# Gated scan and top-2 mixture of experts in fp32: the output products of an expert as seven block products, and one accumulator bank for z

## The chip, the core and the metric

The kernel runs on one core of one Trainium2 chip. The metric is the device time in microseconds (us) of one execution, lower is better; the time of a version is the median of its runs. A profile is one further execution, recorded instruction by instruction.

## The reference, cut to what matters

Two layers, each with a residual, on x of shape (8, 1024, 256), all in fp32. The first is a normalised gated linear scan. The second is a mixture of experts: 8 groups of 1024 tokens, 8 experts, each token goes to its two best experts, and each expert takes C = 256 places per group.

```
x = x + attn(layernorm(x))                 # projections, scan along the tokens
xn = layernorm(x)
expert_inputs  = einsum('GSEC,GSM->EGCM', dispatch, xn)         # M = 256
hidden         = gelu(einsum('EGCM,EMH->EGCH', expert_inputs, w0)) * einsum('EGCM,EMH->EGCH', expert_inputs, w1)
expert_outputs = einsum('EGCH,EHM->EGCM', hidden, wo)           # H = 1368
x = x + einsum('EGCM,GSEC->GSM', expert_outputs, combine)
```

The change is in the line of expert_outputs.

## The kernel before, in words

**Blocks, units, sets.** The 8 groups are worked in 4 blocks (n = 0 to 3) of 2 groups. A unit is one expert on one block, 32 units in all. H = 1368 is 11 chunks of 128 channels (the last has 88), and a set is two chunks of a unit: 6 sets per unit, s = 0 to 5, where s = 5 has the one chunk of 88. That makes 192 sets, worked in order by `run_set`. A *product* below is one `nc.tensor.matmul`; in fp32 it is two TensorE instructions in the trace.

**The w0 and w1 products.** For the two weights and the two groups, `run_set` forms four results with seven block products instead of eight (a Strassen-like scheme in Winograd's form). The sums of weights come from GpSimd (`row_sums`), the sums of inputs from VectorE (`column_sums`). Three of the partial results share one accumulating bank, z: TensorE writes `z a11`, ScalarE copies the bank to SBUF (snap0), TensorE adds `z s2`, ScalarE copies (snap1), TensorE adds `z s3`, ScalarE copies (snap2), TensorE adds `z a22`, and VectorE reads the bank a last time. Each step must wait until the copy before it is done. Other products stand between the steps: `p_a`, `p_b`, and the output products of the set before.

**The output products.** `outputs(st, part)` is called four times per set (group 0 or 1, first or second 128 places), each time with one product per chunk, so eight products in a full set and four in s = 5. It uses hid with places on the output partitions, so that the result in bank py is already stored as rows. The products of one set are issued in the next one: part 0 ahead of `z s2`, part 1 ahead of `z s3`, parts 2 and 3 ahead of `z a22`.

**VectorE in a set,** in the order written: c11 = snap0 + p_a (L750), the second gate of the set before (L729, completes group 1 of hid), snap2 + p_b (L766), the last read of z (L772, completes group 0 of hid), snap1 + p_b (L722).

**Everything else is fed in by `pump`,** twice per set: ahead of parts 2 and 3, and at the end. The list `plan` gives steps of the next block's attention, routing and gating (blocks 0 to 2), of the combination of the block before (blocks 1 to 3), and at fixed sets `gather_unit`, `input_channels` (transposes of the next unit's inputs, s = 3 and 4) and `column_sums` (at the end of s = 4 and in the middle of s = 5). One step can put up to 8 one-hot comparisons (L452) on VectorE. From the first set on the order on every engine is the written one (`manual_schedule`), and each engine works its own queue in that order.

**PSUM** has eight banks: z 2, pa 1, pb 1, py 2, aside 2 (transposes and everything from `pump`).

Of the kernel before, what the change touches and what calls it, by code (L numbers as in the profile page):

```python
# [8 lines left out]
FP = mybir.dt.float32  # L9
# [8 lines left out]
def kernel(  # L18
# [11 lines left out]
    nc = tc.nc  # L30
# [30 lines left out]

    BANKS = {"z": 2, "pa": 1, "pb": 1, "py": 2, "aside": 2}

    def bank(tag, name):
        return psum.tile([P, 512], FP, tag=tag, name=name, bufs=BANKS[tag])

# [5 lines left out]
    def ps_first(name):  # L72
        turn[0] += 1
        return bank(("z", "py", "pa", "z", "py", "pb")[turn[0] % 6], name)

# [4 lines left out]
    nc.scalar.dma_start(wr, router_w.rearrange("(c p) e -> p c e", p=P))  # L80
    wq_sb = pa.tile([P, 3 * KC, D], FP, tag="wq_sb", name="wq_sb")

# [6 lines left out]
    def load_w(b, e, s):  # L89
        lo, w = s * 2 * P, SW[s]  # L90
        a = wpool.tile([P, 2, KC, 2 * P], FP, tag="w01", name=f"w01_{b}_{e}_{s}")
        nc.sync.dma_start(a[:, 0, :, :w], w0[e, :, lo : lo + w].rearrange("(k p) h -> p k h", p=P))
        nc.sync.dma_start(a[:, 1, :, :w], w1[e, :, lo : lo + w].rearrange("(k p) h -> p k h", p=P))
        return a
# [10 lines left out]
    with tc.manual_schedule(engines={mybir.EngineType.SP}):  # L105
        xts = {0: load_x(0)}
        nc.sync.dma_start(wq_sb, w_qkva.rearrange("(c p) d -> p c d", p=P))
        for u in range(1, 3):
            xts[u] = load_x(u)
# [27 lines left out]
    for k in range(KC):  # L137
        for half in range(2):
            pw = ps_first(f"pw_{k}_{half}")
            for c in range(3):  # L140
                nc.tensor.transpose(
                    pw[:, c * P : (c + 1) * P],
                    wq_sb[:, half * 3 + c, k * P : (k + 1) * P],
                    ident,
                )
            nc.scalar.activation(
                wT[:, k, half * 3 * P : (half + 1) * 3 * P], pw[:, : 3 * P],
                AF.Copy, scale=gam[:, k : k + 1],
            )
# [44 lines left out]
    def unit_steps(u, ps):  # L194
# [86 lines left out]
        def second_norm():  # L281
            xn = pa.tile([P, UT, D], FP, tag="xn", name=f"xn_{u}", bufs=2)
            scale_rows(xn, xts.pop(u), t["mv"], t["r"][:, 0, :])
            nc.sync.dma_start(
                xn_d[b][hf * U : (hf + 1) * U, :].rearrange("(i p) d -> p i d", p=P), xn
            )
            t["xn"] = xn
# [32 lines left out]
    def gate_steps(n):  # L320
# [57 lines left out]
        def positions():  # L378
            m, mc = v["m"], v["mc"]
            pos_ps = ps_a(f"pos_{n}")[:, : 2 * T * NE]  # L380
            v["pos_ps"] = pos_ps
            nc.tensor.matmul(pos_ps, lhsT=before, rhs=m.rearrange("p r t e -> p (r t e)"),
                             start=True, stop=False)
            nc.tensor.matmul(pos_ps, lhsT=ones, rhs=mc[:, :, :, :TPG, :], start=False, stop=True)
            cnt_ps = ps_a(f"cnt_{n}")
            nc.tensor.matmul(cnt_ps[:, : GB * NE], lhsT=ones, rhs=mc[:, 0, :, TPG, :],
                             start=True, stop=True)
            cnt = ten("cnt", [P, GB, NE])
            V.tensor_scalar(cnt.rearrange("p g e -> p (g e)"), cnt_ps[:, : GB * NE],
                            float(CAP), None, ALU.min)  # L390

# [62 lines left out]

        def tokens(gl, part):
            tn = v["tn"]
            if part == 0:
                v["ptok"] = ps_a(f"ptok_{n}_{gl}")
            ptok = v["ptok"]
            for q in range(part * 8, part * 8 + 8):  # L460
                r, j = divmod(q, TPG)
                at = hot.pop((gl, q))
                for hh in range(NH):
# [5 lines left out]
                    )  # L469
            if part == 1:  # L470
                pk = ptok[:, : NH * 2 * NE].rearrange("p (h k e) -> p h k e", h=NH, k=2)
                td = pg.tile([P, NH, NE], FP, tag="td", name=f"td_{n}_{gl}")
                V.tensor_scalar(td, pk[:, :, 0, :], float(P), None, ALU.mult)
                V.tensor_tensor(tok[n][:, gl], td, pk[:, :, 1, :], ALU.add)

        steps = [softmax, softmax_sum, lambda: top(0), lambda: top(1), counts, positions, places]
        parts = [(gl, q) for gl in range(GB) for q in range(2)]
        ahead = [lambda gl=gl, q=q: one_hot(gl, q) for gl, q in parts]
        prods = [lambda gl=gl, q=q: tokens(gl, q) for gl, q in parts]
        steps.append(ahead[0])  # L480
        for i in range(len(parts)):
            if i + 1 < len(parts):
                steps.append(ahead[i + 1])
            steps.append(prods[i])
        return steps

    def combine_steps(n):
# [4 lines left out]
        def spare_rows():  # L492

            r = []
            for pool, tag, k in ((pb, "xc", 2), (pa, "h", 1), (pa, "oT", 1), (pa, "xnT", 1)):
                for i in range(k):
                    t = pool.tile([P, UT, D], FP, tag=tag, name=f"far_{tag}_{i}", bufs=k)
                    r += [t[:, q, :] for q in range(UT)]
# [54 lines left out]
    def last_expert_steps():  # L553
# [14 lines left out]
        def by_slot(u, j):  # L568
            if j == 0:
                places_of[u] = pa.tile(  # L570
                    [P, NH, U], FP, tag=("hT", "xn")[(u - lo) // 2], name=f"places_{u}", bufs=2
                )
# [15 lines left out]
    def add_last_expert(u, ot):  # L588
        b, hf = divmod(u, UPG)
        for j in range(2):  # L590
            pc = bank(("z", "aside")[j], f"pc_{u}_{j}")
            for i in range(2):
# [60 lines left out]
    def row_sums(j):  # L653
# [11 lines left out]
        sums[j] = a11, a12, a22, s1, s2, s3, s4  # L665

    class Set:

# [25 lines left out]
    ys = {}  # L694

    def outputs(st, part):

        gl, hh = divmod(part, 2)
        n, e, s, hs = st.n, st.e, st.s, st.hs
        if part % 2 == 0 and s == 0:  # L700
            ys[n, e, gl] = bank("py", f"py_{n}_{e}_{gl}")
        po = ys[n, e, gl]
# [6 lines left out]
        if part % 2 == 1 and s == NS - 1:  # L709
            g = n * GB + gl  # L710
            ot = pb.tile([P, NH, D], FP, tag="ot", name=f"ot_{n}_{e}_{gl}")
            nc.scalar.copy(ot.rearrange("p h d -> p (h d)"), ys.pop((n, e, gl)))
            if (n, e) == units[-1]:
                ys[gl] = ot
                return
            nc.sync.dma_start(
                y_d[g][e * CAP : (e + 1) * CAP, :].rearrange("(h p) d -> p h d", p=P), ot
            )

    def first_sum(st):  # L720
# [9 lines left out]

    def run_set(j, last, pump):

# [4 lines left out]
        nm = f"{st.n}_{st.e}_{st.s}"  # L737
        z, p_a = bank("z", f"z_{nm}"), bank("pa", f"pa_{nm}")
        st.hid = pb.tile([P, GB, 2, CAP], FP, tag="hid", name=f"hid_{nm}", bufs=3)
        st.h2 = st.hid.rearrange("p g c s -> p g (c s)")  # L740
        zz = st.cut(z)

        st.mm(z, a11, b11, True)
# [7 lines left out]
        if last:  # L751
            second_gate(last)
        if last:
            outputs(last, 0)
        st.mm(z, s2, t2, False)
        st.snap1 = st.ten("snap", "sn1", 4)
        A.copy(st.snap1, zz)  # L757
        A.activation(c11, c11, AF.Gelu_apprx_tanh)
        p_b = st.pb = bank("pb", f"pb_{nm}")
        st.mm(p_b, s1, t1, True)  # L760
        if last:
            outputs(last, 1)
        st.mm(z, s3, t3, False)
        snap2 = st.ten("snap", "sn2", 4)
        A.copy(snap2, zz)  # L765
        V.tensor_tensor(st.h2[: st.hs, 1, st.wide], snap2, st.cut(p_b), ALU.add)  # L766
        pump()
        if last:
            outputs(last, 2)
            outputs(last, 3)  # L770
        st.mm(z, a22, t4, False)
        V.tensor_tensor(st.h2[: st.hs, 0, st.wide], zz, c11, ALU.mult)  # L772
        st.mm(p_b, s4, b22, False)
        first_sum(st)
        pump()
        return st

# [65 lines left out]
    with tc.manual_schedule():  # L843
        last, late = None, [[] for _ in range(UB)]
        for n in range(NB):
# [6 lines left out]
            if n > 0:  # L852
                for i, (fetch, add) in enumerate(combine_steps(n - 1)):
                    plan.setdefault(6 + 5 * i, []).append(fetch)
                    plan.setdefault(8 + 5 * i, []).append(add)
            if n == NB - 1:
                for i, f in enumerate(last_expert_steps()):
                    plan.setdefault(8 + 2 * i, []).append(f)
                for i, (fetch, add) in enumerate(combine_steps(n)):
                    k = PUMPS - 2 * NS + 2 + i * 10 // 16  # L860
                    plan.setdefault(k, []).append(fetch)
                    if k + 5 < PUMPS - 1:
                        plan.setdefault(k + 5, []).append(add)
# [4 lines left out]
            def pump():  # L868
# [5 lines left out]
                if nxt in units:  # L874
                    if half == 0 and s == 0 and e + 1 < NE:
                        gather_unit(*nxt)
                    if half == 1 and s == 3:
                        input_channels(*nxt, 0)
                    if half == 0 and s == 4:
                        input_channels(*nxt, 1)  # L880
                    if s == (4, 5)[1 - half]:
                        column_sums(*nxt, 1 - half)
                at[0] += 1

            for j in range(n * NE * NS, (n + 1) * NE * NS):
                if j + 1 < len(sets):
                    row_sums(j + 1)
                st = run_set(j, last, pump)
                load_set(j + AHEAD)
# [39 lines left out]
```

## Time and profile before

| what | value |
|---|---|
| median of 3 runs | 2067.75 us (2064.25 to 2068.35) |
| the profiled execution | 2035.41 us, span 2033.6 us |
| mean granted TensorE clock in it | 0.99 |
| TensorE matmuls busy | 1994.8 us (98%), 9412 instructions |
| VectorE, ScalarE, GpSimd busy | 1056.7, 632.6 and 866.3 us |
| output products (L704) | 2816 instructions, 706.0 us |
| w0/w1 products into z, pa and pb (L682) | 4928 instructions |

How to read it: engines are named PE (TensorE matmul), PEld (TensorE weight load), DVE (VectorE), ACT (ScalarE), POOL (GpSimd) and SP. Matmuls overlap, so the duration of one (381 ns for 256 columns) is longer than the distance from one to the next. Row "idle before" of a group of instructions is the time in which the engine stood still just before them.

### The profile page before, as it was taken

What the parts mean: (1) busy time and instruction counts of PE and PEld (TensorE: products, weight loads), DVE (VectorE), ACT (ScalarE), POOL (GpSimd) and SP (SyncE); (2) the same over time, 40 slices, a digit from 0 to 9 for tenths busy, and PEclk for the clock granted to TensorE, in tenths of its full rate; (3) what the DMA queues carried; (4) which work ended last, traced back from release to release, by engine and by line L of the source; (5) the groups of instructions that cost most, each with busy time, mean ns of one, the idle gap of its engine ahead of it and who ended that gap; (6) DMA issues with size and microseconds to landing.
All of it is one profiled execution on the core that took longest, in us unless ns stands there. A gap on an engine that the chain in (4) does not pass through costs nothing.

```text
span 2033.6 us, 26826 instructions
## 1 busy us (share of the span) xinstructions
PE 1994.8 (98%) x9412; PEld 1658.4 (82%) x9412; DVE 1056.7 (52%) x2114; ACT 632.6 (31%) x1188; POOL 866.3 (43%) x1150
## 2 busy tenths in 40 slices
PE   8889999999999999999999999999999999999998
PEld 4568888888888888888788888888888888888887
DVE  4565354456545454546644554545564454554455
ACT  3222333332333322333332333333322333333331
POOL 2333243333334443545433454444433454444546
PEclk9889999999999999999999999999999999999999
DMA  5231433323332433443423344243334334253433
GB/s 181 73 114 54 123 109 94 111 76 99 103 103 91 135 98 115 134 126 112 148 68 99 124 130 135 80 144 105 116 107 119 119 112 136 86 161 100 139 119 99
DMA packets 224052, 228.80 MB, mean 113 GB/s; under 512 B 32432, under 2 KB 215728, under 8 KB 223920
## 3 DMA queue, kind: packets, MB, share of 16 engines
q1 hardware_dynamic: 211088, 193.51, 31.1%
q0 software_dynamic: 12288, 33.57, 5.7%
q8 instruction: 77, 1.26, 0.3%
q14 instruction: 55, 0.45, 0.1%
q10 hardware_dynamic: 544, 0.01, 0.0%
HBM read 185.61 MB, written 41.42 MB: 112 GB/s over the span
## 4 chain that ended last, share of the span: by engine, by line
PE 93%; DVE 4%; issue 1%; POOL 1%; ACT 1%; DMA 0%; ACTq 0%; DVEq 0%
PE z L682 29%; PE py L704 29%; PE pb L682 15%; PE pa L682 7%; PE pa L235 2%; PE pkv L235 2%; PE pq L235 2%; PE pl L301 1%; PE px L630 1%; PE po L268 1%; PE pc L594 1%; PE pt_h L185 1%; PE pt_x L185 1%; DVE oneh L452 0%; DVE y L255 0%
## 5 line engine op out<-in xcount | busy, mean ns | idle before, releaser
L704 PE MATMUL py<-wo,hid 128*128 128x256 f32 (+1 forms) x2816 | 706.0, 381 | 8.3 <-DVE hid L729 4.8
L704 PEld LDWEIGHTS py<-wo,hid 128*128 128x128 f32 (+1 forms) x2816 | 529.1, 190 | 99.0 <-issue 14.3
L661 POOL TENSOR_TENSOR sb<-w 128x256 f32<-128x256 f32 x188 | 129.5, 689 | 764.6 <-PE pb L682 758.7
L766 DVE TENSOR_TENSOR hid<-sn,pb 128x512 f32<-128x512 f32 x192 | 123.3, 642 | 535.4 <-ACT sn L765 534.4
L682 PE MATMUL z<-tb,sb 128*128 128x256 f32 (+1 forms) x1408 | 366.8, 379 | 0.1
L682 PEld LDWEIGHTS z<-tb,sb 128*128 128x128 f32 (+1 forms) x1408 | 262.7, 187 | 39.8 <-POOL sb L663 0.5
L745 ACT COPY sn<-z 128x512 f32<-128x512 f32 x192 | 105.4, 549 | 598.3 <-PE z L682 598.3
L772 DVE TENSOR_TENSOR hid<-z,c 128x512 f32<-128x512 f32 x192 | 123.7, 644 | 176.7 <-PE z L682 175.9
L750 DVE TENSOR_TENSOR c<-sn,pa 128x512 f32<-128x512 f32 x192 | 122.5, 638 | 128.4 <-PE pa L682 91.3
L757 ACT COPY sn<-z 128x512 f32<-128x512 f32 x192 | 105.3, 549 | 257.7 <-PE z L682 257.7
L682 PE MATMUL z<-xT,w 128*128 128x256 f32 (+1 forms) x704 | 184.9, 381 | 0.0
L682 PE MATMUL z<-tb,w 128*128 128x256 f32 (+1 forms) x704 | 184.6, 381 | 0.2 <-ACT sn L765 0.2
L682 PE MATMUL pb<-tb,sb 128*128 128x256 f32 (+1 forms) x704 | 183.3, 379 | 0.0
L682 PE MATMUL pa<-xT,w 128*128 128x256 f32 (+1 forms) x704 | 183.3, 379 | 0.0
L682 PE MATMUL pb<-xT,sb 128*128 128x256 f32 (+1 forms) x704 | 183.3, 379 | 0.0
L765 ACT COPY sn<-z 128x512 f32<-128x512 f32 x192 | 105.2, 548 | 215.1 <-PE z L682 215.1
L682 PEld LDWEIGHTS z<-tb,w 128*128 128x128 f32 (+1 forms) x704 | 130.6, 187 | 22.7 <-ACT sn L765 3.9
L682 PEld LDWEIGHTS pb<-tb,sb 128*128 128x128 f32 (+1 forms) x704 | 131.6, 187 | 20.3
L682 PEld LDWEIGHTS pa<-xT,w 128*128 128x128 f32 (+1 forms) x704 | 131.7, 187 | 20.3
L682 PEld LDWEIGHTS pb<-xT,sb 128*128 128x128 f32 (+1 forms) x704 | 131.6, 187 | 20.4
L682 PEld LDWEIGHTS z<-xT,w 128*128 128x128 f32 (+1 forms) x704 | 126.8, 188 | 24.8 <-issue 9.1
L729 DVE TENSOR_TENSOR hid<-hid,c 128x512 f32<-128x512 f32 x192 | 143.4, 747 | 3.3 <-ACT c L725 3.3
(150 smaller groups left out, 2312.4 us busy)
## 6 DMA issues: line engine op xcount, KB each, us to landing
w<-in_L_ffn_w_kernel_dram SPq DMA_DIRECT2D x320, 256.0 KB
wo<-in_L_ffn_wo_kernel_dram SPq DMA_DIRECT2D x160, 256.0 KB
y<-ot SPq DMA_DIRECT2D x62, 256.0 KB
xt<-in_L_attn_x_dram SPq DMA_DIRECT2D x16, 512.0 KB
x<-xt SPq DMA_DIRECT2D x16, 512.0 KB
xn<-xn SPq DMA_DIRECT2D x16, 512.0 KB
xc<-x SPq DMA_DIRECT2D x16, 512.0 KB
out_dram<-xc SPq DMA_DIRECT2D x12, 512.0 KB
```

The costliest lines, as they stand in the source:

```text
L185: nc.tensor.transpose(pt[:, i * P : (i + 1) * P], src[:, i, k * P : (k + 1) * P], ident)
L235: nc.tensor.matmul(pp, lhsT=wT[:, k, c * P : (c + 1) * P], rhs=t["hT"][:, k, :], start=(k == 0), stop=(k == KC - 1),)
L661: eng.tensor_tensor(s1, a21, a22, ALU.add)
L682: nc.tensor.matmul(ps[:hs, i * CAP : (i + 1) * CAP], lhsT=a[:, i * hs : (i + 1) * hs], rhs=b, start=first and i == 0, stop=True, skip_grou ...
L704: nc.tensor.matmul(po[:, hh * D : (hh + 1) * D], lhsT=st.hid[:hs, gl, i, hh * P : (hh + 1) * P], rhs=wos[st.j][:hs, i, :], start=(s == 0 a ...
L729: nc.vector.tensor_tensor(h22, h22, st.c12, ALU.mult)
L745: A.copy(snap0, zz)
L750: V.tensor_tensor(c11, snap0, st.cut(p_a), ALU.add)
L757: A.copy(st.snap1, zz)
L765: A.copy(snap2, zz)
L766: V.tensor_tensor(st.h2[: st.hs, 1, st.wide], snap2, st.cut(p_b), ALU.add)
L772: V.tensor_tensor(st.h2[: st.hs, 0, st.wide], zz, c11, ALU.mult)
```

## The change

For a full set of every unit but the last two, the output products become block products too. Channels of the result are on the partitions; the two halves of wo's 256 columns, the two chunks and the two groups make seven products of 128x128 by 128x256. GpSimd makes the four sums of wo blocks (`out_sums`), VectorE makes four sums of hid blocks (`hid_sums`), which need both groups of hid. The seven products accumulate over the five full sets in four banks y0 to y3; s = 5 adds its one chunk by four plain products. After that, `join_outputs` combines the four banks (one ScalarE copy, five VectorE additions) into yT, `output_rows` transposes yT back (four transposes per group, in the sets s = 1 and s = 2 of the next unit), and ScalarE copies the rows. The last two units of the last block (`plain`) keep the old form.

PSUM is now z 1, pa 1, pb 1, y0 to y3 four, aside 1. The output products stand elsewhere in the set: two ahead of `z s2` (none where the set before has s = 0), none between `p_b` and `z s3`, there `between` puts transposes in s = 1 to 4, one ahead of `z a22` (three where the set before has s = 0; two plain ones where it has s = 5), four behind it. `input_channels` moves from `pump` to `between`. Further: the weights w01 have 7 buffers in place of 8, xn has 1 in place of 2, both w_qkva halves are loaded into the buffers xc, the one-hot steps of gating are no longer one step ahead of their products, the positions are copied out of PSUM by ScalarE, and some late steps move by a few pumps.

```diff
-    BANKS = {"z": 2, "pa": 1, "pb": 1, "py": 2, "aside": 2}
     def bank(tag, name):
-        return psum.tile([P, 512], FP, tag=tag, name=name, bufs=BANKS[tag])
+        return psum.tile([P, 512], FP, tag=tag, name=name, bufs=1)
...
+    def out_sums(j):
...
+        eng = nc.gpsimd
+        eng.tensor_tensor(s1, a21, a22, ALU.add)
+        eng.tensor_tensor(s2, s1, a11, ALU.subtract)
+        eng.tensor_tensor(s3, a11, a21, ALU.subtract)
+        eng.tensor_tensor(s4, a12, s2, ALU.subtract)
...
+    def hid_sums(st):
...
+        V = nc.vector
+        V.tensor_tensor(t1, b12, b11, ALU.subtract)
+        V.tensor_tensor(t2, b22, t1, ALU.subtract)
+        V.tensor_tensor(t3, b22, b12, ALU.subtract)
+        V.tensor_tensor(t4, b21, t2, ALU.subtract)
...
+            add_product(st, name, *{
+                "p1": (a11, b11), "p2": (a12, b21), "p6": (s2, t2), "p5": (s1, t1),
+                "p7": (s3, t3), "p4": (s4, b22), "p3": (a22, t4),
+            }[name])
...
+        early = [f["p1"], f["p2"]]
+        late = [f["p6"], f["p7"], f["p5"], f["p3"], f["p4"]]
+        if st.s == 0:
+            return [], [], early + late
+        return early, [], late
...
     def run_set(j, last, pump, between):
...
-        if last:
-            outputs(last, 0)
+        for f in early:
+            f()
         st.mm(z, s2, t2, False)
...
+        if last and last.j in osums_of:
+            hid_sums(last)
         st.mm(p_b, s1, t1, True)
-        if last:
-            outputs(last, 1)
+        between()
         st.mm(z, s3, t3, False)
...
+        for f in middle:
+            f()
         pump()
-        if last:
-            outputs(last, 2)
-            outputs(last, 3)
+        for f in late[:-4]:
+            f()
         st.mm(z, a22, t4, False)
         V.tensor_tensor(st.h2[: st.hs, 0, st.wide], zz, c11, ALU.mult)
+        for f in late[-4:]:
+            f()
         st.mm(p_b, s4, b22, False)
         first_sum(st)
+        if last and last.s == NS - 1 and not plain(last.n, last.e):
+            join_outputs(last)
         pump()
...
                 if j + 1 < len(sets):
                     row_sums(j + 1)
-                st = run_set(j, last, pump)
+                out_sums(j)
+                st = run_set(j, last, pump, between)
```

## The prediction

> **What bounds the kernel now.** I read the page first: busy times, the chain that ended last, the costliest groups with their idle time.
>
> ```profile
> PE 1994.8 (98%) x9412; PEld 1658.4 (82%) x9412; DVE 1056.7 (52%) x2114; ACT 632.6 (31%) x1188; POOL 866.3 (43%) x1150
> PE 93%; DVE 4%; issue 1%; POOL 1%; ACT 1%; DMA 0%; ACTq 0%; DVEq 0%
> L704 PE MATMUL py<-wo,hid 128*128 128x256 f32 (+1 forms) x2816 | 706.0, 381 | 8.3 <-DVE hid L729 4.8
> L766 DVE TENSOR_TENSOR hid<-sn,pb 128x512 f32<-128x512 f32 x192 | 123.3, 642 | 535.4 <-ACT sn L765 534.4
> ```
>
> TensorE is the chain, and it waited 8.3 us in all ahead of 2816 output instructions. VectorE waits 535 us for the third snapshot alone. So two things price the change: TensorE instructions added or removed, and any wait that now reaches TensorE's own queue. For the first, the timeline of TensorE:
>
> ```profile
> 1561.73 1.03 PE L682 MATMUL z<-tb,sb 128*128 128x256 f32 x4
> 1562.59 1.89 PE L704 MATMUL py<-wo,hid 128*128 128x256 f32 x8
> 1564.32 1.03 PE L682 MATMUL z<-tb,w 128*128 128x256 f32 x4
> 1565.18 1.03 PE L682 MATMUL pb<-xT,sb 128*128 128x256 f32 x4
> 1566.04 0.60 PE L630 MATMUL px<-ident,xg 128*128 128x128 f32 x4
> 1566.48 1.03 PE L682 MATMUL z<-xT,w 128*128 128x256 f32 x4
> ```
>
> By distance from start to start: eight instructions take 1564.32-1562.59 = 1.73 us, so a product (two) takes 0.4325 us; four transposes take 0.44 us. The fence also shows the old cover: between `z s3` and `z a22` stand four products, 1.73 us, in which snap2 is copied. For the second, the first set of all, which has no output products, shows a snapshot with less cover (whole timeline; the bracket is idle time and its end):
>
> ```profile
> 138.09 1.03 PE L682 MATMUL pa<-xT,w 128*128 128x256 f32 x4
> 138.29 0.58 ACT L745 COPY sn<-z 128x512 f32<-128x512 f32 x1 [0.47 <-PE z L682]
> 139.02 1.10 PE L682 MATMUL z<-tb,sb 128*128 128x256 f32 x4
> 139.96 1.03 PE L682 MATMUL pb<-tb,sb 128*128 128x256 f32 x4
> 140.16 0.58 ACT L757 COPY sn<-z 128x512 f32<-128x512 f32 x1 [1.28 <-PE z L682]
> ```
>
> From `p_a` to `p_b` it took 139.96-138.09 = 1.87 us where four products cost 1.73. Two products of cover (0.865) are 0.14 us short. The need is 0.20 (from the first covering instruction to the copy's start) + 0.58 + about 0.14 (copy's end to the next product) = 0.92 us. With one product of cover the stall is 0.92-0.43 = 0.49 us, with none 0.92; in s = 5, whose copy takes 0.37, it is 0.28 with one.
>
> **What the Trainium skill says.** "PSUM — Partial Sum Buffer", section "PSUM bank collisions raise a hardware error", asks that engines be kept apart by whole bank; so z's next product waits for the copy of the bank, as the 0.14 us show. "GPSIMD Engine Reference", section "Specifications", says that GpSimd shares SBUF interfaces with VectorE, contended when VectorE has two SBUF inputs. The trace agrees; the groups by shape have the same subtraction at two places of a set:
>
> ```profile
> L646 DVE TENSOR_TENSOR tb<-xT 128x256 f32<-128x256 f32 x32 | 19.5, 609 | 0.0
> L649 DVE TENSOR_TENSOR tb<-xT 128x256 f32<-128x256 f32 x32 | 13.7, 429 | 0.0
> ```
>
> L646 runs at a set's start, beside `row_sums`, L649 in the middle.
>
> **The change part by part.** Thirty units change, two stay plain.
>
> Products. Each of 5 full sets has seven in place of eight: 150 x 0.4325 = 64.9 us less. In s = 5 four stay four. The transposes back are 30 x 8 x 0.11 = 26.4 us more. Net **-38.5 us** on TensorE. ScalarE gets one copy per unit and GpSimd 600 sums of 128x128 (a 128x88 one takes 0.39, so about 0.45 each, 270 us in all, to some 56% busy); GpSimd does them after the next `row_sums`, a set ahead of use. Both cost nothing themselves, covered by TensorE's set of about 10 us. VectorE gets 600 `hid_sums` at 0.43 to 0.61; I take 0.5 (300 us), the ends being two rows just shown. Five joining additions per unit (two at 0.42, three at 0.69: 2.9 us, 87 us) follow. VectorE goes to about 1445 us, 70%.
>
> A. The third snapshot in s = 2, 3, 4. One product (p6) covers it unless the middle `pump` has TensorE work. In the written order, each cover at its distance, the shortfalls add to 20.1 us in the 72 sets of blocks 0 to 2 and 8.1 us in the 18 of block 3: **28 us**. Queued behind are p7, p5, p3, p4 and the rest of TensorE.
>
> B. s = 5, the short set: 14 products, 6.05 us. snap1 has one product of cover (`p_b`): 0.28. Then VectorE is late. Its order, in the set before the change (its end shows when hid is complete):
>
> ```profile
> 1576.62 0.69 DVE L722 TENSOR_TENSOR c<-sn,pb 128x512 f32<-128x512 f32 x1 [0.17 <-PE pb L682]
> 1577.22 0.45 DVE L646 TENSOR_TENSOR tb<-xT 128x256 f32<-128x256 f32 x1
> 1577.71 0.84 DVE L647 TENSOR_TENSOR tb<-xT,tb 128x256 f32<-128x256 f32 x1
> 1578.47 0.41 DVE L750 TENSOR_TENSOR c<-sn,pa 88x256 f32<-88x256 f32 x1
> 1578.80 0.88 DVE L729 TENSOR_TENSOR hid<-hid,c 128x512 f32<-128x512 f32 x1
> ```
>
> The set's first product is at 1576.42. hid is complete 3.26 us later, and p6 needs the second of four `hid_sums`, at 4.3 us. TensorE is at p6 after seven products and the stall, 7 x 0.4325 + 0.28 = 3.3 us. Stall 1.0, with the 0.28 **1.3 us** per unit in the light case. With the average of pump work ahead (1 us more on VectorE at the end of s = 4, 0.9 more in the middle of s = 5, which delays L772 and so the single z bank) it is about 2.3. Light everywhere: 38 us; 2.3 in the 24 units of blocks 0 to 2: 63. I take **50**.
>
> C. s = 0 and s = 1. In s = 0 the snapshots have two products (0.1 in all), and after `z a22` only two products stand ahead of the next `z a11`, which needs L772 (0.20+0.69+0.14 against 0.865): 0.16. Then VectorE has L722, the join until about 3.6 us into s = 1, c11, the second gate and two `hid_sums`, to 6.1; TensorE waits for yT (0.2) and again at p6 (0.3 to 0.4), and snap0 is short by 0.07. Together 0.9 per unit light, 1.5 with average pumps: 26 to 41 us, I take **33**.
>
> D. Plain units: parts 2 and 3 now stand after `z a22`, so snap2 has none but the pump. The same count gives **11 us** for 12 sets.
>
> E. Heavy pumps. Eight one-hots are 8 x 0.343 = 2.7 us on VectorE; a normal set hides about 2 us of pump work at either place. Twelve such steps and the placing of tokens would cost up to 15 us, nothing if they fall well: **7**.
>
> The single aside bank lets a transposition of `between` wait for the pump's step before it, usually read half a set earlier; 0 to 5 us, taken within E. Ahead of the sets and at the end (seven rotating banks for six, one xn buffer, two `add` steps moved past the last set, 1.0 us on VectorE and 3.3 on GpSimd) I take +2, from -3 to +6. SP issues the same loads and stores, the stores of rows over a set later, the loads queued behind them six sets ahead of use; w01's seventh buffer is free when asked for. Nothing.
>
> Sum: 28+50+33+11+7+2-38.5 = +92.5 us on the profiled 2035.4, 2128. The median shown is 32 us above that execution; the difference is added to it: 2067.75+92.5 = **2160**.
>
> **The rivals.** First, *only the bank waits*: VectorE never makes TensorE wait. By the same count over all sets the shortfalls are 36.0 (blocks 0 to 2) + 12.7 + 11.0 = 60 us, so 2067.75+60-38.5 = 2089. For it: VectorE's 535 us of waiting. Against: the order shown in B.
>
> Second, *VectorE becomes the bound* in blocks 0 to 2: if `hid_sums` take 0.61 and more beside a busier GpSimd, B and C reach their upper ends and A's sets stall at p6 too. 63+41+28+11+15+2-38.5 = +121, and 150 x 0.44 us (four sums 0.11 longer) = 66 at most on top: 2190 to 2250, say 2215.
>
> Third, *faster*: p6 as a cover. It comes out on that side if TensorE's new waits stay below 38.5 us, 0.2 us per set. That needs the pump's attention products to fill nearly all of A in blocks 0 to 2, and VectorE to be at p6 in time in s = 5 and s = 1. Then 8 (block 3) + 11 + 10 (snap1 in s = 5) = 29 remain: 2058. For it: pumps with TensorE work fill most of those gaps in the order. Against: the count in A includes them already.
>
> That the block form is not executed is excluded: the written order of the changed kernel has 1258 output products where 1408 stood, and 240 transposes more.
>
> **How the numbers follow.** The stated account 0.62 (its own range 2125 to 2195), only bank waits 0.14, VectorE bound 0.14, faster 0.10. The range 2085 to 2215 leaves out the faster case and the upper part of the second rival. A difference of 0.2% (4 us) is about what a measurement of this kernel can tell from none: faster 0.09, within it 0.02, slower 0.89.
>
> **What would show it.** Right: TensorE busy down by about 38 us but its idle time up by over 100; a new idle entry of tens of us at `z a22` ended by the third snapshot (A, D), at the first of the seven products ended by a VectorE tw (B, C), and at `z a11` ended by VectorE's last read of z; sets s = 5 longer than 7 us where 6.05 are products. VectorE near 70%. Wrong: TensorE still without waits (then faster by the full 38 us), or waits on GpSimd's so or sb, or the transposes back well over 0.11 us each.

## The result, and the profile after

The changed kernel takes **2204.39 us** (median of 4 runs, 2199.97 to 2204.91) against 2067.17 us of the kernel before: ratio 1.066 (95% interval 1.064 to 1.068), **137 us slower**. It is a loss in the direction forecast; 44 us more than the forecast 2160 and inside its range.

The page of the changed kernel, the same parts as were read of before:

```profile
PE 2039.6 (93%) x9352; PEld 1619.8 (74%) x9352; DVE 1454.0 (66%) x2862; ACT 642.8 (29%) x1222; POOL 1194.8 (54%) x1754
PE 76%; DVE 14%; ACT 3%; issue 3%; another core or an unknown queue 1%; DMA 1%; POOL 1%; ACTq 0%; SPq 0%; DVEq 0%; POOLq 0%
L755 PE MATMUL acc<-tw,so 128*128 128x256 f32 x900 | 254.1, 392 | 48.0 <-DVE tw L767 47.8
L703 PE MATMUL z<-tb,w 128*128 128x256 f32 (+1 forms) x704 | 195.9, 398 | 30.0 <-ACT sn L885 29.5
L703 PE MATMUL z<-xT,w 128*128 128x256 f32 (+1 forms) x704 | 189.1, 388 | 18.5 <-DVE hid L893 17.7
L886 DVE TENSOR_TENSOR hid<-sn,pb 128x512 f32<-128x512 f32 x192 | 122.5, 638 | 171.5 <-ACT sn L885 166.8
```

TensorE is no longer the whole chain: VectorE has 14% of it and ScalarE 3%. The three TensorE rows name the waits by the tile that was late: tw (the second of `hid_sums`, ahead of p6, the first of the seven products that reads such a sum), sn (the third snapshot, ahead of `z a22`), hid (the last read of the single z bank, ahead of the next `z a11`). In the kernel before, the output products idled for 8.3 us in all, and the two z rows not at all:

```profile
L682 PE MATMUL z<-xT,w 128*128 128x256 f32 (+1 forms) x704 | 184.9, 381 | 0.0
L682 PE MATMUL z<-tb,w 128*128 128x256 f32 (+1 forms) x704 | 184.6, 381 | 0.2 <-ACT sn L765 0.2
```

VectorE's spare time ahead of the sum that reads the third snapshot (L766 before, L886 now) fell from 535 to 172 us.

The timeline of TensorE in a set s = 2 of the last block, where the pump has no TensorE work:

```profile
1713.29 1.03 PE L703 MATMUL z<-tb,sb 128*128 128x256 f32 x4
1714.16 0.59 PE L755 MATMUL acc<-tw,so 128*128 128x256 f32 x2
1715.05 1.13 PE L703 MATMUL z<-tb,w 128*128 128x256 f32 x4 [0.30 <-ACT sn L885]
1716.02 1.03 PE L755 MATMUL acc<-tw,so 128*128 128x256 f32 x4
```

p6 alone covers the snapshot. From its start to `z a22` are 0.89 us instead of 0.43: a loss of 0.46 (forecast 0.49). The bracket shows 0.30 only, since a matmul's record is longer than the distance to the next one; distances from start to start are the surer reading.

VectorE and TensorE in s = 5 of the same unit, each from its own timeline:

```profile
1738.95 0.69 DVE L839 TENSOR_TENSOR c<-sn,pb 128x512 f32<-128x512 f32 x1 [1.84 <-PE pb L703]
1739.55 0.45 DVE L643 TENSOR_TENSOR tb<-xT 128x256 f32<-128x256 f32 x1
1740.04 0.84 DVE L644 TENSOR_TENSOR tb<-xT,tb 128x256 f32<-128x256 f32 x1
1740.80 0.41 DVE L870 TENSOR_TENSOR c<-sn,pa 88x256 f32<-88x256 f32 x1
1741.13 0.88 DVE L846 TENSOR_TENSOR hid<-hid,c 128x512 f32<-128x512 f32 x1
1742.05 0.83 DVE L766 TENSOR_TENSOR tw<-hid 128x256 f32<-128x256 f32 x1
1742.92 0.43 DVE L767 TENSOR_TENSOR tw<-hid,tw 128x256 f32<-128x256 f32 x1
```

```profile
1741.62 0.64 PE L703 MATMUL z<-tb,sb 128*88 128x256 f32 x2
1742.09 0.60 PE L573 MATMUL pt_s<-ident,sent 128*128 128x128 f32 x4
1743.49 0.67 PE L755 MATMUL acc<-tw,so 128*128 128x256 f32 x2 [0.80 <-DVE tw L767]
```

The set began at 1738.74. VectorE ends the second sum at 1743.35 and p6 starts 0.14 us later, 4.75 us into the set; with four transposes ahead of it TensorE was ready at 1742.53. Two column sums (L643, L644) stand ahead of the second gate (L846) on VectorE, as the prediction read them in the kernel before.

For the experiments I use one more figure: the time from the first `z a11` to the start of the last unit but one. That is 180 sets, the 30 units that change. Taken from the starts in the trace it is **1769.9 us before and 1902.9 after** (+133.0; 1899.2 in a second profile of the changed kernel). It leaves out the last unit, in which most profiles have one stop of TensorE of some 26 us that the shown profile of before has not (2035 us against 2067 in its runs); on one of the chips no version profiled there had it, and the kernel before took 2036 us there. So lengths are compared in the 180 sets, and ratios to the kernel before on the same chip.

Sums over equal positions of a set in these 180, in us:

| kernel | s = 0 | 1 | 2 | 3 | 4 | 5 | all |
|---|---|---|---|---|---|---|---|
| before | 271.7 | 312.3 | 319.8 | 322.5 | 323.5 | 220.1 | 1769.9 |
| after | 287.8 | 340.6 | 331.9 | 341.4 | 325.1 | 276.1 | 1902.9 |

The short set s = 5 has 56 of the 133 us.

### The profile page after: what moved, and what is told of

Its sections match the earlier page's. It is cut to its first block, busy times and chain, and to the rows that moved or that the text cites. A ratio compares the mean times of both kernels' runs of the same rounds, so it can differ in the third digit from the quotient of the medians.

```text
span 2203.1 us, 28099 instructions
## 1 busy us (share of the span) xinstructions
PE 2039.6 (93%) x9352; PEld 1619.8 (74%) x9352; DVE 1454.0 (66%) x2862; ACT 642.8 (29%) x1222; POOL 1194.8 (54%) x1754
## 4 chain that ended last, share of the span: by engine, by line
PE 76%; DVE 14%; ACT 3%; issue 3%; another core or an unknown queue 1%; DMA 1%; POOL 1%; ACTq 0%; SPq 0%; DVEq 0%; POOLq 0%
PE z L703 24%; PE acc L755 20%; PE pb L703 11%; PE pa L703 6%; PE pa L237 2%; PE pq L237 2%; ACT sn L885 2%; PE pkv L237 2%; DVE hid L846 2%; PE py L735 2%; DVE tw L766 1%; PE pl L303 1%; DVE c L870 1%; DVE tw L767 1%
## 5 line engine op out<-in xcount | busy, mean ns | idle before, releaser
L703 PE MATMUL z<-tb,sb 128*128 128x256 f32 (+1 forms) x1408 | 375.5, 386 | 21.4 <-issue 16.4
L865 ACT COPY sn<-z 128x512 f32<-128x512 f32 x192 | 105.4, 549 | 796.9 <-PE z L703 778.2
L703 PEld LDWEIGHTS z<-tb,sb 128*128 128x128 f32 (+1 forms) x1408 | 247.0, 188 | 81.6 <-issue 31.4
L755 PE MATMUL acc<-tw,so 128*128 128x256 f32 x900 | 254.1, 392 | 48.0 <-DVE tw L767 47.8
L839 DVE TENSOR_TENSOR c<-sn,pb 128x512 f32<-128x512 f32 x192 | 123.2, 642 | 255.6 <-PE pb L703 250.1
L755 PEld LDWEIGHTS acc<-tw,so 128*128 128x128 f32 x900 | 170.4, 195 | 92.3 <-issue 38.2
L886 DVE TENSOR_TENSOR hid<-sn,pb 128x512 f32<-128x512 f32 x192 | 122.5, 638 | 171.5 <-ACT sn L885 166.8
L703 PE MATMUL z<-tb,w 128*128 128x256 f32 (+1 forms) x704 | 195.9, 398 | 30.0 <-ACT sn L885 29.5
L755 PE MATMUL acc<-hid,wo 128*128 128x256 f32 x840 | 217.6, 382 | 0.6 <-DVE hid L846 0.6
L703 PE MATMUL z<-xT,w 128*128 128x256 f32 (+1 forms) x704 | 189.1, 388 | 18.5 <-DVE hid L893 17.7
L877 ACT COPY sn<-z 128x512 f32<-128x512 f32 x192 | 105.5, 550 | 280.7 <-PE z L703 257.1
L755 PEld LDWEIGHTS acc<-hid,wo 128*128 128x128 f32 x840 | 159.3, 191 | 26.7 <-issue 2.9
L846 DVE TENSOR_TENSOR hid<-hid,c 128x512 f32<-128x512 f32 x192 | 149.2, 777 | 4.7 <-ACT c L842 4.5
```

What stands on the lines that cost most here:

```text
L703: nc.tensor.matmul(ps[:hs, i * CAP : (i + 1) * CAP], lhsT=a[:, i * hs : (i + 1) * hs], rhs=b, start=first and i == 0, stop=True, skip_grou ...
L755: nc.tensor.matmul(ys[n, e, i][:, half * CAP : (half + 1) * CAP], lhsT=lhsT, rhs=rhs, start=fresh, stop=True, skip_group_check=True,)
L839: nc.vector.tensor_tensor(st.c12, st.snap1, st.cut(st.pb), ALU.add)
L846: nc.vector.tensor_tensor(h22, h22, st.c12, ALU.mult)
L865: A.copy(snap0, zz)
```

## The experiments

**The cover of the snapshots, alone, in the kernel before** (before_parts_behind).

```diff
-        if last:
-            outputs(last, 2)
-            outputs(last, 3)
         st.mm(z, a22, t4, False)
         V.tensor_tensor(st.h2[: st.hs, 0, st.wide], zz, c11, ALU.mult)
+        if last:
+            outputs(last, 2)
+            outputs(last, 3)
```

> The kernel before with one edit: output parts 2 and 3 (four products) stand behind z a22 in place of ahead of it, so that only the pump's work covers the third snapshot; z keeps two banks, no instruction is added. Theory (a snapshot needs 0.92 us of cover): 0.92 us in each full set whose middle pump has no TensorE work, 0.5 where it has a few transposes, 0.7 in s = 5: 70 to 120 us slower than the kernel before, about 2160. Rival (the snapshots cost nothing while z has two banks): within 15 us of it.

2170.11 us, ratio 1.051 (1.049 to 1.053): 105 us slower, 92.5 in the 180 sets. The row of `z a22`, which idled for 0.2 us in the kernel before:

```profile
L682 PE MATMUL z<-tb,w 128*128 128x256 f32 (+1 forms) x704 | 200.3, 404 | 76.4 <-ACT sn L765 74.0 <-issue 2.3
```

Moving four products of the old form from ahead of `z a22` to behind it costs 5%, with two z banks and no work added. The rival is out.

**More cover in the changed kernel** (split_late): `late[:-4]` and `late[-4:]` become `late[:-2]` and `late[-2:]`.

> The changed kernel with three of the seven products (five where the set before has s = 0) ahead of z a22 and two behind it, in place of one (three) and four. Theory (snapshots short of cover, VectorE late): with three products, 1.30 us, in front of the 0.92 us need the wait of z a22 for the third snapshot goes in the sets s = 2 to 5, some 0.46 us in each set where the pump has no TensorE work; part comes back as waits of p7 and p5 for their VectorE sums. 15 to 35 us faster than the changed kernel, about 2180. Rival (VectorE alone is what is late): the products wait for the same sums, only earlier; within 5 us or slower. Rival (the one z bank between sets): only two products ahead of p_b's last one now cover the last read of z; slower by 10 us or more.

2176.63 us, 1.054 (1.052 to 1.056); 180 sets 1873.6, 29 us less. s = 2, 3 and 4 fell by 9, 7 and 12 us, s = 5 by 3, s = 0 not at all.

```profile
L703 PE MATMUL z<-tb,w 128*128 128x256 f32 (+1 forms) x704 | 189.8, 389 | 12.0 <-ACT sn L885 11.9
L755 PE MATMUL acc<-tw,so 128*128 128x256 f32 x900 | 231.6, 393 | 49.2 <-DVE tw L767 47.7 <-DVE tw L768 1.2
```

The wait for the snapshot fell from 30.0 to 12.0, the one for tw stayed. The row of `z a11` idled no longer than before (17.9 us against 18.5), so two products behind `z a22` are enough for the last read of z. The waits for ScalarE and for VectorE are two separate losses.

**Without the sums of hid** (no_hid_sums).

```diff
-        V.tensor_tensor(t1, b12, b11, ALU.subtract)
-        V.tensor_tensor(t2, b22, t1, ALU.subtract)
-        V.tensor_tensor(t3, b22, b12, ALU.subtract)
-        V.tensor_tensor(t4, b21, t2, ALU.subtract)
-        st.t = t1, t2, t3, t4
+        st.t = b12, b12, b22, b22
```

> The changed kernel without the four VectorE sums of hid (600 instructions, 340 us of VectorE time); the products that used them read hid of group 1 itself, which needs the second gate all the same. Left out of the computation: these sums. Theory: the waits in s = 5 (0.9 us of 1.3 to 2.3 per unit) and at p6 in s = 1 go, and the last reads of z come sooner; the short covers of the third snapshot stay. 60 to 95 us faster than the changed kernel, about 2125. Rival (waits for the banks are the whole cost): within 20 us. Rival (VectorE is the bound throughout blocks 0 to 2): 120 us or more faster, back to the kernel before or below it.

2142.39 us, 1.037 (1.036 to 1.039), 62 us less than the changed kernel's 2204; 180 sets 1841.8 (-61): 39 of it in s = 5, 14 in s = 3, 7 in s = 1. That is at the low end of what the theory gave, far from what "VectorE is the bound" gave: with 300 us less on VectorE the kernel is still 77 us slower than before. VectorE is late at certain places; it is not full.

**The column sums out of the way** (colsums_later).

```diff
-                    if s == (4, 5)[1 - half]:
-                        column_sums(*nxt, 1 - half)
+                    if s == 5:
+                        column_sums(*nxt, half)
```

> The changed kernel with the four VectorE sums of the next unit's inputs (column_sums) in the middle and at the end of s = 5, in place of the end of s = 4 and the middle of s = 5. Theory (B: VectorE reaches hid_sums late in the short set s = 5 because 1.1 us of column sums stand ahead of them): the wait of p6 in s = 5 shrinks by about 1 us per unit, part of it given back where the last sums now stand ahead of s = 0; 15 to 30 us faster than the changed kernel (2204), about 2180. Rival (the waits in s = 5 are for the snapshots, whatever VectorE does): within 5 us.

2159.18 us on the chip without the stop, 1.060 (1.059 to 1.062); 180 sets 1883.3, 20 less: s = 5 fell by 22.1, s = 0 rose by 5.6. The row `acc<-tw,so` now idles for 31.2 us in place of 48.0. So VectorE's written order in s = 5 is the cause of 22 of the 56 us that this set lost, of which 6 come back in s = 0.

**A shorter join** (short_join): the additions of L815, L816 and L822 are left out, the other two read the ScalarE copy and one bank each.

> The changed kernel with two of the five joining additions (512 columns each), 1.4 us of VectorE in place of 2.9 per unit. Left out of the computation: three additions, so that parts of the accumulators are not read. Theory (C: the join delays VectorE in s = 1, and p6 and the transposes wait): up to 1.5 us less wait in s = 1 per unit, s = 0 unchanged: 15 to 35 us faster than the changed kernel. Rival (in s = 1 the pump's work and the snapshots set the time): within 5 us.

2157.02 us, 1.060 (1.058 to 1.062); 180 sets 1881.3, 22 less, and all of it in s = 1 (340.6 to 318.3). 1.5 us less on VectorE gave 0.74 us per unit. The starts in the trace show where: of the 22 us, 8 were the wait at p6 and 12.5 those of the pump's products and transposes.

**Without the sums of wo** (no_out_sums): GpSimd's four subtractions and additions are left out.

> The changed kernel without the 600 GpSimd sums of wo blocks (about 347 us of GpSimd time); the products read blocks of wo instead. Left out of the computation: these sums. Theory (the cost is covers and VectorE's order): hid_sums run 0.43 in place of 0.57 us where GpSimd no longer works beside them, and the few waits on GpSimd (some 30 us on the weight loads' row) go: 10 to 30 us faster than the changed kernel. Rival (GpSimd's sharing of SBUF with VectorE is the main cost): 60 us or more faster.

2152.92 us, 1.058 (1.056 to 1.060); 180 sets 1875.0, 28 less: 13 in s = 3, 8 in s = 1, 4 in s = 5. Two of the four groups of `hid_sums`, first with GpSimd's sums, then without (the line numbers are six lower there):

```profile
L766 DVE TENSOR_TENSOR tw<-hid 128x256 f32<-128x256 f32 x150 | 87.7, 585 | 5.2
L767 DVE TENSOR_TENSOR tw<-hid,tw 128x256 f32<-128x256 f32 x150 | 83.0, 554 | 5.2
```

```profile
L760 DVE TENSOR_TENSOR tw<-hid 128x256 f32<-128x256 f32 x150 | 75.0, 500 | 5.2
L761 DVE TENSOR_TENSOR tw<-hid,tw 128x256 f32<-128x256 f32 x150 | 71.7, 478 | 5.2
```

GpSimd's sums, which "cost nothing themselves" in the prediction, lengthen each of these VectorE sums by some 0.08 us. Without them the two rows still take 0.48 to 0.50 us, not the 0.43 that the theory named. The Trainium skill, "GPSIMD Engine Reference", section "Specifications", says that the two engines contend when VectorE has two inputs in SBUF, and these rows agree. The theory's range held, just.

**Two banks for z** (two_z_banks).

```diff
-    ACC = {..., "p4": (3, 0), "x": (3, 1)}
+    ACC = {..., "p4": (2, 0), "x": (2, 1)}
...
+        return psum.tile([P, 512], FP, tag=tag, name=name, bufs=2 if tag == "z" else 1)
```

> The changed kernel with z in two banks again; for that p4 and the fourth product of s = 5 are added into the bank y2, on top of p7 and p5, so that y3 is free. Wrong sums, the same instructions. Theory: only the wait of z a11 for the last read of z goes, 18 us on TensorE's row and up to 43 with the weight loads': 15 to 40 us faster, the largest part in s = 0 and s = 5. Rival (the single z bank is the main cost of the change): 80 us or more faster.

2199.67 us, 1.065 (1.063 to 1.067): 5 us less, and 1897.6 in the 180 sets, which is 5 us below the one profile of the changed kernel and 2 below the other. A miss of the theory. The wait at `z a11` is gone (idle 18.5 to 0.0), s = 0 is 13.4 us shorter, and s = 1 is 17.6 us longer: TensorE only meets the same late VectorE a set later. By its starts, the waits at the transposes of yT grew from 0.4 to 6.9 us, those of the pump's products and transposes in s = 1 from 14.0 to 19.6, and `p_b` waits 4.4. In the changed kernel that bank alone is not what costs.

**One bank for z in the kernel before** (before_one_z): `"z": 1` in BANKS.

> The kernel before with z in one bank, nothing else. Theory: between a22 and the next a11 only the two products of p_b (0.865 us) cover the last read of z, 1.03 us: 0.16 us per set, 31 us in all, more where the pump's VectorE work stands ahead of the read, in full sets of blocks 0 to 2: 40 to 90 us slower than the kernel before. Rival (one bank for z costs little, as two_z_banks gave back 5 us only): within 15 us.

2105.04 us, 1.020 (1.018 to 1.021): 40 us slower, 31 in the 180 sets, at the lower edge of what was expected.

```profile
L682 PE MATMUL z<-xT,w 128*128 128x256 f32 (+1 forms) x704 | 195.4, 396 | 17.0 <-DVE hid L772 14.7 <-DVE xt L274 0.8 <-issue 0.3
```

Where TensorE had almost no other waits, the second bank is worth 2%. In the changed kernel giving it back was worth a quarter of a percent at most, since other waits stand behind it.

**Two banks for aside** (two_aside_banks): as two_z_banks, but for aside; after_again ran beside it.

> The changed kernel as it is, for the pieces run beside it: 1.060 to 1.072 of the kernel before.

2201.63 us, 1.067 (1.065 to 1.069).

> The changed kernel with aside in two banks again, made free as in two_z_banks (p4 and the fourth product of s = 5 added into y2; wrong sums, the same instructions). Theory (the prediction priced the single aside bank too low): TensorE's starts in the changed kernel's trace show some 29 us of delay ahead of pump products and transposes in s = 1, 3 and 4, where a transposition of between stands half a set ahead in the same bank; 20 to 30 us faster than after_again. Rival (these are VectorE's lateness and would show elsewhere): within 8 us.

2189.73 us, 1.060 (1.059 to 1.062), 12 us less than after_again. By the total it lies between theory and rival. The trace parts it: ahead of the sets and in the first of them the order of the steps came out differently (transposes of the attention now stand between the first products of the first set), and the second set starts at 155.9 us in place of 143.4, 12.5 us lost. From there to the last unit but one it is 1867.5 us against 1890.6 in after_again: 23 us gained, as the theory had it, 11 of it in s = 1 and 14 in s = 3, with 4 lost in s = 5. The pump's projections no longer wait for the copy of a transposed bank:

```profile
L237 PE MATMUL pa<-hT,wT 128*128 128x512 f32 x128 | 68.2, 658 | 7.5 <-ACT ot L719 4.8 <-DVE xT L630 2.3 <-ACT hT L190 0.5
```

```profile
L237 PE MATMUL pa<-hT,wT 128*128 128x512 f32 x128 | 66.5, 647 | 1.1 <-DVE xT L630 0.6 <-ACT hT L190 0.5
```

(The first is the changed kernel, the second two_aside_banks.)

**The products placed by their covers** (reordered).

```diff
+        ahead, behind = [f["p4"], f["p5"], f["p6"]], [f["p7"], f["p3"]]
+        if st.s == 0:
+            return [], [], [f["p1"], f["p2"]] + ahead, behind
+        return [f["p1"]], [f["p2"]], ahead, behind
```

> The changed kernel, complete, with its products placed so that each snapshot has at least 0.86 us of cover: p1 ahead of z s2, p2 ahead of z s3, p4, p5, p6 ahead of z a22, p7 and p3 behind it; in s = 0 the four plain products two ahead of z a22 and two behind; in plain units one output part at each of four places, as in the kernel before. Theory (A, D and the short covers in s = 0): what split_late gained (28 us) and some 10 us in the plain units, 5 in s = 0: 35 to 55 us faster than the changed kernel, about 2160, and still slower than the kernel before by 4 to 5%, since VectorE's lateness stays. Rival (covers were nearly the whole loss): 100 us or more faster, to the kernel before or below it.

2114.94 us on the chip without the stop, 1.039 (1.038 to 1.041), and 58 us less in the 180 sets (1844.8): more than expected, 25 us of it in s = 5, where p4 and p5 now stand in the time until p6's sum is there. Part of the wait moved with them: the row of p4, `acc<-hid,so`, idles for 19.3 us where it had no idle time.

```profile
L755 PE MATMUL acc<-tw,so 128*128 128x256 f32 x900 | 250.6, 387 | 2.3 <-DVE tw L767 0.7 <-DVE tw L766 0.2
L703 PE MATMUL z<-tb,w 128*128 128x256 f32 (+1 forms) x704 | 188.4, 387 | 1.9 <-ACT sn L886 1.7
```

**Both placings** (reordered_colsums).

> reordered and colsums_later together, complete. Theory: covers and VectorE's order in s = 5 are separate losses and add: some 15 us faster than reordered (1.039 of the kernel before), about 1.031. Rival (both took away the same wait at p6 in s = 5): within 5 us of reordered.

2121.18 us, 1.028 (1.026 to 1.030); 180 sets 1830.1, 14.7 less than reordered, of the 19.6 that colsums_later gave alone. They add for the most part, as the theory had it. It is the best complete form of the change that was run, and it is still 60 us longer than the kernel before in these sets: no version that was run beats that kernel.

## Why the prediction was right, and what it mis-sized

The sign, the main mechanism and the range held; the size did not. The forecast change was 92.5 us and the measured one 137, and three terms were too small (B, C, E) and none clearly too large, so no errors cancelled. To compare term by term I took, from the starts of TensorE's instructions in the trace, how much later each started than the usual distance behind its predecessor. In the sets this is 20.9 us before and 230.1 after, 26.3 of them the stop in the last unit. 230.1-26.3-20.9 = 183 us of new waits, less the 38.5 of saved products, is 144; the spans differ by 169.5-26.3 = 143. In the 180 sets alone, without the stop, my count of the waits is 17.7 before and 190.0 after: 172.3 less 38.5 is 133.8, and the sets differ by 133.0. In reordered and reordered_colsums the same balance comes out within 1 us. So **the saving of 38.5 us** is consistent with the rest; it wasn't measured by itself.

The trace column below holds all waits of the changed kernel but the stop. Of the 20.9 us that were there before, about 7 belong to s = 5 and 8 to s = 0 and 1.

| term | forecast | trace |
|---|---|---|
| products and transposes | -38.5 | fits the balance |
| A: `z a22` in s = 2, 3, 4 | 28 | 30.8 |
| B: s = 5 | 50 | 69.0 |
| C: s = 0 and 1, without aside | 33 | 48.5 |
| D: plain units, without the stop | 11 | 13 |
| E: heavy pumps, with aside | 7 | 42, of it 29 ahead of pump products and transposes |

**A and D** were right to a few us: the need of 0.92 us, read from one set of the kernel before, held where one product covers the snapshot (0.46 us lost in the set shown), and split_late and before_parts_behind show the mechanism by itself. The reading of two products was less good. The prediction calls them 0.14 us short, but by its own need they are 0.92-0.865 = 0.055 short, and it used that smaller figure in C. In its lines `z s2` starts 0.065 us late; the rest of the 0.14 lies within `z s2` itself.

**B** was mis-sized by 19 us. Of the 69 us, about 50 stand at p6 and the products just behind it. Per unit the trace has 1.8 us in block 3 (forecast 1.3 for light pumps) and 2.5 in blocks 0 to 2 (forecast 2.3 for average ones). `hid_sums`, taken at 0.50 us, last 0.57 on average, which is part of that; and midway between light and average pumps was too low: the average case (63) was nearer. no_hid_sums (39 us less in s = 5) shows that these waits are for VectorE, and colsums_later that 22 us of them come from its order.

**C** was mis-sized by 15. The forecast put 0.16 us per unit, 5 us, on the next `z a11`; 16 us in all stood there. That the pump's VectorE work ahead of the last read of z was counted in its average only would explain it, but no run varied that alone. The snapshots with two products of cover lost 11 us in s = 0 and 1, where the forecast has 5. two_z_banks shows that freeing the wait at `z a11` gives next to nothing, since s = 1 grows by as much, and short_join that the join is what holds s = 1.

**E** is the step that failed. "0 to 5 us, taken within E" was said of the single aside bank, on the ground that the bank is "usually read half a set earlier". The prediction looked at one direction only, a transposition of `between` that waits for the pump's step before it; those transpositions wait for 2.8 us in all (1.9 before). The other direction it put at nothing: the pump's TensorE step comes about 1 us behind the transposition and waits for its copy. That is 29 us by the trace, 14.0 in s = 1 and 12.5 in s = 3 for the most part, and 23 us come back in two_aside_banks. `between` puts a transposition into that bank in four of six sets, and in s = 1 and s = 3 its copy often stands behind other work of VectorE or ScalarE. The very pump work that covers a snapshot now starts late.

It takes both, the one bank and a late copy. With the one bank kept, the pump's waits in s = 1 fall to 1.5 us in short_join, and those in s = 3 to 2.4 in no_hid_sums and 4.0 in no_out_sums; with two banks all of them fall to 1.6. So the gains of these four runs overlap and can't be added up. no_out_sums also shows a second term that was put at nothing: GpSimd's sums cost 28 us. That they do so by way of VectorE fits the shorter rows there, but isn't shown by itself. The other 13 us of E may come from the one-hot steps or from the other moves listed with the change; no run tried these by themselves.

One of the named signs did not come: TensorE's busy time was to fall by 38 us and rose from 1994.8 to 2039.6, with 60 instructions fewer. The records of the waiting rows are longer (398 and 388 ns on average where 381 stood), so busy time of TensorE does not show what was saved.

The rivals: "only the bank waits" (2089) is excluded by no_hid_sums, whose 61 us it can't hold; "faster" needed under 38.5 us of new waits and there were 183. "VectorE becomes the bound" named a time (2215) closer than the main one. Its upper ends for B and C (63 and 41) are closer too, and `hid_sums` did lengthen. But what sets it apart isn't there: in s = 2, 3 and 4 the products of `hid_sums` wait for only about 3 us in all, VectorE's busy share is 66%, and taking 300 us from it returned 61.

## What to carry to other kernels

Before a product is removed from a saturated TensorE queue, ask what it stood in front of: here leaving out 150 products was worth 65 us by the count, and moving four products per set away from the bank copy that they covered cost 105 (before_parts_behind). Place work by what it waits for and what it covers, those operands that are ready first into the gap that opens first; that alone took back 58 of 133 us. A buffer that is shared by two streams is to be priced in both directions, and by the time from its use to its release in the busiest queue, not on average.

## What the runs showed of the hardware that was not expected

In the last unit, while GpSimd issues 28 indirect loads in one row (32 in the kernel before), TensorE stopped in most of the profiles. After `p_b` was issued at 2132.00 in the changed kernel (timeline of all engines):

```profile
2132.00 1.03 PE L703 MATMUL pb<-tb,sb 128*128 128x256 f32 x4
...
2148.84 0.58 ACT L877 COPY sn<-z 128x512 f32<-128x512 f32 x1 [18.60 <-remote]
...
2149.47 2.07 PE L703 MATMUL z<-tb,sb 128*128 128x256 f32 x4 [16.45 <-issue]
```

TensorE's next product, `z s3`, needs the copy of L877, and ScalarE began that copy 16.8 us after `p_b`; elsewhere it is some 0.2 us. The profile names no instruction of this core that ScalarE waited for. The third snapshot of the set was late too: ScalarE idled for 8.72 us ahead of it, and `z a22` started at 2159.30. The granted clock was 0.76 in the stretch from 2120 to 2150 us and 0.74 from 2150 to 2175, against 1.00 on both sides. Its record goes to 0.5 at 2135.5, some 3 us after TensorE's last start, so the slower clock came after the stop had begun. While it lasted, four instructions took 2.07 us in place of 1.03.

That set took 36.9 us where its neighbours took 10.6. It ended only after the last of these loads was issued (2154.0). On one chip four versions of the change did not show the stop, and the time of the kernel before there (2036 us) leaves no room for it. The same instructions run with and without it, so it isn't part of the change; its cause was not tried and stays open.
